# A two-layer graph network: Strassen's second level in o and two more groups, three banks for seven products, and another order of the last group

## The chip, the cores and the metric

The kernel runs on one core of a Trainium2 chip. The core's engines take their instructions in order, each from a queue of its own: TensorE multiplies matrices, VectorE, ScalarE and GpSimd work on elements, SyncE issues the transfers. TensorE writes its results into the accumulators (PSUM), 8 banks of 512 float32 columns in 128 partitions. VectorE and ScalarE read them there. The metric is the device time of one execution in microseconds (us), the median over several runs. All data are float32.

## The reference

x has 64 batches of 256 tokens and 512 features; adj is a 256x256 matrix with zeros and values up to 1. Both layers add their result to x:

```
h = relu(layernorm(x));  x = x + (adj @ h) @ W0 + b0
h = relu(layernorm(x));  q, k, v = h @ Wq + bq, h @ Wk + bk, h @ Wv + bv      (8 heads of 64)
s = q k^T / 8 + (1 - adj) * -1e9;  x = x + softmax(s) v @ Wo + bo
```

The softmax runs over the 256 keys of each head and batch.

## The kernel before

**Groups.** Two batches make a group (GB = 2, NG = 32 groups). Layer 0 runs over all groups and leaves the residual and the transposed hidden state in DRAM; then layer 1 runs over them. In layer 1 the second half of one group is interleaved with the first half of the next. In the loop from line 970 on, iteration g does: attend(g, 0), load_residual(g), load_hidden(g+2), score(g, 1), q and k of group g+1, attend(g, 1), score(g+1, 0), v of g+1, then post(g), which is the product with Wo (o). attend takes four of the eight heads (qd = 0 or 1): the sums over keys (pden), attention times v (pav), and later divide. The last iteration has no next group: it runs post(30) between attend(31, 0) and attend(31, 1), and post(31) at the end.

**Strassen's product.** For a group, w (layer 0), q, k, v and o are each a 512x512 weight times 512 tokens. They are computed by seven products of half size (project, line 447), by Winograd's form: sums of weight quarters (s1 to s4, weight_sums) against differences of the activations' halves (t1 to t4, class Halves, made by GpSimd). Each half product is four matmuls of 128x128 against 128x256 (product, line 439) into one bank. Some products add onto others in a bank: a bank "grows" while VectorE or ScalarE reads its states in between. read() takes a partial sum, finish() completes one quarter of the result.

**The second level.** From group FIRST2 = 4 on, q, k and v use project2 (line 561). Three of the seven half products (a12, s4, a22: those whose result is used in one quarter only) are there computed by Strassen again: seven matmuls of 128x128 against 128x128 in place of eight (product2, line 534). Three or four of the seven write parts of one shared bank, from which VectorE spreads them over the quarters (finish2, line 547). Their weight sums are made once (block_sums, in SBUF that layer 0 has left, `spare`), their activation differences once a group (class Blocks, block_hidden).

**The order of work.** Every step emits its instructions in program order. `after(delay, fn)` puts a function into a list that is due some ticks later, and `tick()`, called after each step of a projection, runs what is due. So a tick decides where, say, a subtraction by GpSimd stands in GpSimd's queue. Banks are taken and given back in first-in, first-out order (bank, give, from line 246 on). The instructions that other parts hang on: top is subtracted from the scores (L846, GpSimd), exp (L851, ScalarE), the key sums `as` (key_sum, L858, GpSimd), which attend's pden needs; reciprocal and product by VectorE in divide (L885, L901); the t sums (L437, GpSimd); bo added to the residual (L978, GpSimd).

**Lines of the page.** L444 is a half product's matmul, L545 a quarter's; L609 is every add of a bank into SBUF by VectorE; L765 and L786 are ScalarE's reads for q, k and for v; L530 to L532 are the differences of the second level. Lines 909 to 915 hold the order of sums and of divide in the last groups:

```
            elif g == NG - 2:
                after(9, HO[g].sums, nc.gpsimd, ("t2", "t3", "t4"))
            else:
                HO[g].sums(nc.vector, ("t2",))
                after(1, HO[g].sums, nc.vector, ("t3", "t4"))

        after(1 if g < NG - 1 or qd else 8, divide)
```

After post(NG-1)'s fourth step the kernel checks its softmax sums for a bound (bad, worst, pf, from line 1004 on) and sets a flag that would start a slower path.

Of the kernel before, what the change touches and what calls it, by code (L numbers as in the profile page):

```python
# [13 lines left out]
P = 128  # L14
# [184 lines left out]
def kernel(  # L199
# [247 lines left out]
    def project(s, halves, by_token, name, read, finish, in_place=False):  # L447

        def new(n):
            return bank([P, 2, N], f"{name}{n}")

        def p1():
            o["a"] = new("a")
            product(o["a"], s, "a11", halves, "b11", by_token, stop=False)
            o["u1"] = read(o["a"], 1)

        def p2():
            pb = new("b")  # L460
            product(pb, s, "a12", halves, "b21", by_token)
            finish(pb, o["u1"], 0, 0)
            give(pb)

        def p3():
            product(o["c"], s, "s4", halves, "b22", by_token, start=False)
            finish(o["c"], o["u2"], 0, 1)
            give(o["c"])

        def p4():  # L470
            pd = new("d")
            product(pd, s, "a22", halves, "t4", by_token)
            finish(pd, o.get("u3"), 1, 0)
            give(pd)

        def p5():
            o["c"] = new("c")
            product(o["c"], s, "s1", halves, "t1", by_token, stop=False)
            o["c22"] = read(o["c"], 0)

        def p6():
            product(o["a"], s, "s2", halves, "t2", by_token, start=False, stop=False)
            o["u2"] = read(o["a"], 2)

        def p7():
            product(o["a"], s, "s3", halves, "t3", by_token, start=False)
            o["u3"] = read(o["a"], 3)
            finish(o["a"], o["c22"], 1, 1)
            give(o["a"])

        o = {}
        for step in (p1, p5, p2, p6, p4, p7, p3) if in_place else (p1, p2, p6, p5, p7, p4, p3):
            step()
            yield

# [5 lines left out]
    FIRST2 = 4  # L501
    W2, spare = {}, []

    def block_sums(n):

        todo = []
        for a in ONCE:
            w = W[n][a]
            def part(i, j):
                return w[:, j, i * P:(i + 1) * P]  # L510
            s1, s2, s3, s4 = (spare.pop(0) for _ in range(4))
            W2[n, a] = dict(a11=part(0, 0), a12=part(0, 1), a22=part(1, 1), s1=s1, s2=s2, s3=s3, s4=s4)
            for o, p, q, op in ((s1, part(1, 0), part(1, 1), ALU.add), (s2, s1, part(0, 0), ALU.subtract),
                                (s3, part(0, 0), part(1, 0), ALU.subtract), (s4, part(0, 1), s2, ALU.subtract)):
                todo.append((nc.gpsimd.tensor_tensor, o, p, q, op))
        return todo
# [17 lines left out]
    def product2(own, shared, s, x, by_token, fresh):  # L534

        q = own.rearrange("p m (n k) -> p (m n) k", k=P)
        c11, c12, c21, c22 = (q[:, i, :] for i in ((0, 2, 1, 3) if by_token else (0, 1, 2, 3)))
        for o, a, b, start in ((shared[:, 0, :], "a11", "b11", True), (shared[:, 1, :], "s2", "t2", False),
                               (shared[:, 2, :], "s3", "t3", False),
                               (c22 if fresh else shared[:, 3, :], "s1", "t1", fresh),  # L540
                               (c11, "a12", "b21", False), (c12, "s4", "b22", False), (c21, "a22", "t4", False)):
            lhs, rhs = s[a], x.operand(b)
            if by_token:
                lhs, rhs = rhs, lhs
            nc.tensor.matmul(o, lhs, rhs, start=start, stop=True, skip_group_check=True)  # L545

    def finish2(o, own, shared, u, by_token, fresh):

        def quarters(t):
            return t.rearrange("p m (n k) -> p (m n) k", k=P)  # L550

        def spread(i, n):
            return shared[:, i:i + 1, :].to_broadcast([P, n, P])
        q = quarters(o)
        lower = q[:, 1::2, :] if by_token else q[:, 2:4, :]
        right = q[:, 2:4, :] if by_token else q[:, 1::2, :]
        return [(o, own, u), (q, spread(0, 4), q), (q[:, 1:4, :], spread(1, 3), q[:, 1:4, :]),
                (lower, spread(2, 2), lower),
                (right[:, 0, :], quarters(own)[:, 3, :], right[:, 0, :]) if fresh else (right, spread(3, 2), right)]

    def project2(n, halves, blocks, by_token, name, read, target):

        s = W[n]

        def new(i):
            return bank([P, 2, N], f"{name}{i}")

        def once(own, a, i, k, u, fresh):
            shared = bank([P, 4, P], f"{name}r")
            product2(own, shared, W2[n, a], blocks[ONCE[a]], by_token, fresh)  # L570
            return own, shared, finish2(target(i, k), own, shared, u, by_token, fresh)

        def finish_all(*products):
            for ops in zip(*(ops for _, _, ops in products)):
                for op in ops:
                    add(*op)
            for own, shared, _ in products:
                give(own)
                give(shared)

        pa = new("a")
        product(pa, s, "a11", halves, "b11", by_token, stop=False)
        u1 = read(pa, 1)
        yield
        pc = new("c")
        product(pc, s, "s1", halves, "t1", by_token, stop=False)
        c22 = read(pc, 0)
        yield
        product(pa, s, "s2", halves, "t2", by_token, start=False, stop=False)
        u2 = read(pa, 2)  # L590
        yield
        c12 = once(pc, "s4", 0, 1, u2, False)
        yield
        c11 = once(new("b"), "a12", 0, 0, u1, True)
        finish_all(c12, c11)
        yield
        product(pa, s, "s3", halves, "t3", by_token, start=False)
        u3 = read(pa, 3)
        add(target(1, 1), pa, c22)
        give(pa)  # L600
        yield
        finish_all(once(new("d"), "a22", 1, 0, u3, True))
        yield

    def partial(name, n):
        return tmp.tile([P, 2, N], F32, tag="u", name=f"u{n}_{name}")
# [4 lines left out]

    RESIDUAL = {0: (1, 1), 1: (0, 0), 2: (0, 1), 3: (1, 0)}
# [30 lines left out]
    def layer0(g):  # L643
# [17 lines left out]
        for d in range(DC):  # L661
# [5 lines left out]
            if d >= 2:  # L667
                halves.sums(nc.gpsimd, ("t1", "t2"), d - 2)
# [9 lines left out]

        def read(ps, n):
            o = quarter(xt, *RESIDUAL[n])  # L680
            add(o, ps, o)
# [20 lines left out]
        def finish(ps, u, i, k):  # L702
            o = quarter(xt, i, k)
            add(o, ps, o)
# [15 lines left out]
        yield from project(W["0"], halves, True, f"w_{g}", read, finish)  # L720
# [14 lines left out]
    def hidden_sums(g, *steps):  # L735

        HH[g] = Halves(f"h_{g}", [H1T[g][:, k] for k in range(GB)], 0 if g else 1)
        for step, n in zip(steps, ("t1", "t2", "t3", "t4")):
            after(step, HH[g].sums, nc.gpsimd, (n,))

    H2 = {}
# [305 lines left out]
```

## Time and profile before

| | us |
|---|---|
| median of 3 runs | 2688.69 (2688.48 to 2688.98) |
| the profiled execution | 2688.09 |
| its span, first to last instruction | 2686.3 |
| TensorE busy (matmuls) | 2659.3 |
| VectorE busy | 1958.6 |
| GpSimd busy | 1960.1 |
| ScalarE busy | 868.9 |

Layer 1 begins about 613 us after the span's start (its first q is interleaved with the end of layer 0), and its groups follow at 63.5 us each from group 4 on. A line of the page names the engine, the operation, what it writes and reads, the shape, the count and the duration. The chain of work is followed backwards from the last instruction: it tells what set the end. A float32 matmul shows as two records of its weight load and two of its product, so x8 on L444 is one half product and x2 on L545 one quarter matmul. Since matmuls are pipelined, the distance of starts is what one costs; the recorded length has the drain in it.

### The profile page before, as it was taken

To read this page: it belongs to the slowest core of one execution; us is meant where nothing else is said; L and a number is where in the kernel's file an instruction comes from. 1 tells how busy PE (TensorE), PEld (TensorE's weight loads), DVE (VectorE), ACT (ScalarE), POOL (GpSimd) and SP (SyncE) were. 2 spreads that over 40 slices of the span, in tenths; PEclk is the share of its full clock that TensorE was granted. 3 is DMA by queue.
4 is the path that set the end of the run, shared out by engine and by line. 5 is a ranking of instruction groups with operands and counts; after the bars stand their busy time and mean duration, and the time that the engine had idled before them with its cause. 6 is when DMAs were issued, how large, how long until landed. Compare 5 with 4: busy or idle time off the path is not lost.

```text
span 2686.3 us, 47911 instructions
## 1 busy us (share of the span) xinstructions
PE 2659.3 (99%) x18684; PEld 2267.5 (84%) x18684; DVE 1958.6 (73%) x3789; ACT 868.9 (32%) x1537; POOL 1960.1 (73%) x1630
## 2 busy tenths in 40 slices
PE   8999999999999999999999999999999999999998
PEld 7888888888788888888888888888888888888886
DVE  7878787875455777777777777777777777777776
ACT  3444344443222233332222233222222333332222
POOL 6777777674777777777777777777777777777775
PEclk9999999999999999999999999999999999999999
DMA  7776666663112221111111111111122211111110
GB/s 188 187 198 162 163 170 166 164 157 97 31 54 61 55 52 48 48 48 48 48 48 48 48 48 48 48 48 48 56 63 63 56 48 48 48 48 48 48 48 33
DMA packets 281047, 210.80 MB, mean 78 GB/s; under 512 B 145904, under 2 KB 212976, under 8 KB 280816
## 3 DMA queue, kind: packets, MB, share of 16 engines
q1 hardware_dynamic: 280352, 207.15, 29.7%
q8 instruction: 150, 2.46, 0.4%
q10 hardware_dynamic: 464, 0.52, 0.1%
q14 instruction: 81, 0.66, 0.1%
HBM read 106.96 MB, written 100.66 MB: 77 GB/s over the span
## 4 chain that ended last, share of the span: by engine, by line
PE 97%; DVE 1%; POOL 1%; DMA 0%; issue 0%; SPq 0%; ACTq 0%; POOLq 0%; DVEq 0%
PE sc L835 8%; PE py L655 8%; PE pav L874 8%; PE pden L867 2%; POOL a L846 1%; DVE v L609 0%; DVE k L609 0%; PE v_29a L444 0%; PE q_29a L444 0%; PE v_28a L444 0%; PE v_27a L444 0%; PE v_25a L444 0%; PE q_25a L444 0%; PE v_24a L444 0%; PE q_23a L444 0%; PE q_21a L444 0%
## 5 line engine op out<-in xcount | busy, mean ns | idle before, releaser
L846 POOL TENSOR_TENSOR a<-a,top 128x1024 f32<-128x1024 f32 x254 | 593.2, 2369 | 512.3 <-DVE a L840 512.3
L840 DVE SCALAR_TENSOR_TENSOR a<-sc,maskT 128x512 f32<-128x512 f32 x512 | 312.0, 682 | 58.1 <-PE sc L835 57.4
L858 POOL TENSOR_TENSOR as<-a 128x512 f32<-128x512 f32 x256 | 319.2, 1281 | 0.7 <-DVE r L691 0.7
L851 ACT ACTIVATE a<-a 128x1024 f32<-128x1024 f32 x256 | 264.1, 1054 | 22.4 <-POOL a L846 22.4
L885 DVE RECIPROCAL den<-den 128x128 f32<-128x128 f32 x256 | 223.7, 919 | 38.0 <-ACT den L881 37.9
L835 PE MATMUL sc<-q,k 64*128 64x256 f32 x2048 | 239.2, 383 | 0.6 <-DVE a L840 0.6
L835 PEld LDWEIGHTS sc<-q,k 64*128 64x128 f32 x2048 | 194.3, 187 | 46.1 <-issue 26.3
L874 PE MATMUL pav<-a,v 128*32 128x256 f32 x4096 | 232.7, 379 | 0.0
L655 PE MATMUL py<-adjT,h 128*128 128x256 f32 x1024 | 228.2, 381 | 0.9 <-DVE adjT L325 0.9
L655 PEld LDWEIGHTS py<-adjT,h 128*128 128x128 f32 x1024 | 195.7, 191 | 28.5 <-ACT h L630 1.2
L874 PEld LDWEIGHTS pav<-a,v 128*32 128x32 f32 x4096 | 133.1, 110 | 87.9
L685 ACT ACTIVATE h<-x,nb,rs 128x512 f32<-128x512 f32 x128 | 97.1, 806 | 318.3 <-POOL nb L54 318.1
L881 ACT ACTIVATE den<-pden 128x512 f32<-128x512 f32 x64 | 38.2, 597 | 493.8 <-PE pden L867 493.1
L53 POOL TENSOR_TENSOR rs<-rs,mhalf 128x2 f32<-128x2 f32 (+1 forms) x97 | 78.8, 812 | 123.7 <-DVE nb L52 123.7
L978 POOL TENSOR_TENSOR x<-x,bo_r 128x512 f32<-128x512 f32 x128 | 159.4, 1277 | 12.2 <-DVE x L609 12.2
L634 POOL TENSOR_TENSOR x<-x,b_r 128x512 f32<-128x512 f32 x128 | 159.1, 1276 | 1.0 <-ACT h L630 0.9
L437 POOL TENSOR_TENSOR t_y<-yT,t_y 128x256 f32<-128x256 f32 (+1 forms) x96 | 87.3, 909 | 41.2 <-ACT yT L665 38.6
L706 DVE BATCH_NORM_STATS2 st<-x 128x6 f32<-128x256 f32 x256 | 96.4, 418 | 4.4
L630 ACT ACTIVATE h<-x,nb,rs 128x512 f32<-128x512 f32 x128 | 93.9, 805 | 10.8 <-POOL nb L54 10.8
L42 DVE BATCH_NORM_STATS2 st<-x 128x6 f32<-128x512 f32 x128 | 85.6, 669 | 7.5 <-DMA x<-in_x_dram 7.5
L437 POOL TENSOR_TENSOR t_y<-yT 128x256 f32<-128x256 f32 (+1 forms) x96 | 88.0, 916 | 2.3 <-ACT yT L665 0.9
L691 DVE STREAM_TRANSPOSE r<-h 128x512 f32<-128x512 f32 x128 | 82.7, 683 | 2.1 <-ACT h L685 1.4
(5610 smaller groups left out, 6381.4 us busy)
## 6 DMA issues: line engine op xcount, KB each, us to landing
x<-in_x_dram SPq DMA_DIRECT2D x256, 128.0 KB, 3.5
residual<-x SPq DMA_DIRECT2D x256, 128.0 KB, 2.3
hidden<-r SPq DMA_DIRECT2D x128, 256.0 KB, 4.6
h1T<-hidden SPq DMA_DIRECT2D x64, 512.0 KB, 9.4
x<-residual SPq DMA_DIRECT2D x32, 1024.0 KB, 6.7
out_dram<-x SPq DMA_DIRECT2D x62, 512.0 KB, 3.2
w_sb<-in_L_gnn_weight_dram SPq DMA_DIRECT2D x1, 1024.0 KB, 6.5
wq_sb<-in_L_gnn_Wq_dram SPq DMA_DIRECT2D x1, 1024.0 KB, 7.7
```

The lines of the kernel that those rows point to most:

```text
L437: eng.tensor_tensor(self.t[n][:, c, :], self.operand(p, c), self.operand(q, c), op=ALU.subtract)
L634: nc.gpsimd.tensor_tensor(xt[:, t, :], xt[:, t, :], b0_r, op=ALU.add)
L655: nc.tensor.matmul(pss[d][:, b * N:(b + 1) * N], h[:, b * NT + k, d * P:(d + 1) * P], adjT[:, k, :], start=(k == 0), stop=(k == NT - 1))
L685: nc.scalar.activation(h1[:, k * NT + t, :], xt[:, k * NT + t, :], AF.Relu, bias=nb[:, t:t + 1], scale=rs[:, t:t + 1])
L835: nc.tensor.matmul(ps[j][:, kt * N:(kt + 1) * N], k[j * HD:(j + 1) * HD, c, kt * P:(kt + 1) * P], q[j * HD:(j + 1) * HD, c, :], start=True ...
L840: nc.vector.scalar_tensor_tensor(a[:, j * NT:(j + 1) * NT, :].rearrange("p k n -> p (k n)"), ps[j], SCALE, maskT_f, op0=ALU.mult, op1=ALU.add)
L846: nc.gpsimd.tensor_tensor(a, a, top_b, op=ALU.subtract)
L851: nc.scalar.activation(a, a, AF.Exp)
L858: nc.gpsimd.tensor_tensor(AS[c, b], a4[:, :, 0, :], a4[:, :, 1, :], op=ALU.add)
L874: nc.tensor.matmul(po[f][h * 32:(h + 1) * 32, b * N:(b + 1) * N], v[:, k, h * HD + f * 32:h * HD + f * 32 + 32], A[h // 2, b][:, (h % 2) * ...
L885: nc.vector.reciprocal(rden[:, c * P:(c + 1) * P], den[:, c * P:(c + 1) * P])
L978: after(9 + t, lambda t, xt: nc.gpsimd.tensor_tensor(xt[:, t, :], xt[:, t, :], L1["o"][1], op=ALU.add), t, X[g])
```

## The change

1. **project** has three banks (pa, pc, pb) and another order: a11, a12, s2, s3, s1, a22, s4. a11, s2, s1 and s4 grow in pa; s3 and a22 in pc; a12 has pb. `put` writes a first value into a quarter of the result (`first`: ScalarE with bias for q and k, a copy for v, an add on VectorE into x for layer 0 and o), `more` adds a bank to it in place.
2. **project2** computes the three inner products in parts: after a11 into pa, s3 into pc and s2 into pa (steps 1 to 3, each read by put) come their a11 products together in step 4 (each into the first 128 columns of a bank of its own), s2 and s3 in step 6, the rest in step 7, and s1 last. The sums grow in those banks, so that VectorE adds each state only to the quarters that want it, and nothing is spread over four.
3. **FIRST2** is 2 instead of 4, and **post** uses project2 from group 2 on (block_outputs, with GpSimd; on VectorE for the last group). Its first value is an add to x on VectorE (add_up).
4. **The inner s3** of a weight is written over the quarter that it is made of. block_sums run at other ticks: q in iteration 0, k and v in iteration 1, o in iteration 2.
5. **t sums** are made in the order t3, t1, t2, t4 (hidden_sums) and t3, t2, t4 (divide); in layer 0, t1 by halves as soon as yT is there.
6. **The last groups**: divide always comes one tick after attend; post(30) is cut at its fifth step by attend(31, 1); sums of o_30 at 5 ticks for 9; OT of the last group lies in the pool of x; only one subtraction of top is left to VectorE, in score(31, 1); that score's key sums and the adds of bo come earlier. exp of a score's fourth part comes two ticks later, except there.
7. **Output**: a batch is sent when its two quarters are complete; in the last group each quarter is sent by itself, and three of the four at the very end.

The core of the diff:

```diff
+        pa = bank([P, 2, N], f"{name}a")
+        product(pa, s, "a11", halves, "b11", by_token, stop=False)
+        put(pa, 0, 0)
+        yield
+        pb = bank([P, 2, N], f"{name}b")
+        product(pb, s, "a12", halves, "b21", by_token)
+        more(pb, 0, 0)
+        give(pb)
+        complete(0, 0)
+        yield
+        product(pa, s, "s2", halves, "t2", by_token, start=False, stop=False)
+        put(pa, 1, 0)
+        yield
+        pc = bank([P, 2, N], f"{name}c")
+        product(pc, s, "s3", halves, "t3", by_token, stop=False)
+        put(pc, 1, 1)
+        yield
+        product(pa, s, "s1", halves, "t1", by_token, start=False, stop=False)
+        more(pa, 1, 1)
+        complete(1, 1)
+        yield
+        product(pc, s, "a22", halves, "t4", by_token, start=False)
+        more(pc, 1, 0)
...
+        product(pa, s, "s4", halves, "b22", by_token, start=False)
+        put(pa, 0, 1)
...
-    FIRST2 = 4
+    FIRST2 = 2
...
+    def project2(n, halves, blocks, by_token, name, place, first, done=None, add_up=False):
...
+        for a, i, k, own in (("a12", 0, 0, None), ("a22", 1, 0, pc), ("s4", 0, 1, pa)):
+            inner.append(Inner(a, i, k, own, bank([P, 2, P], f"{name}{i}{k}")))
+            inner[-1].u1()
+        p2, p4, p3 = inner
+        for p in inner:
+            if p is not p3 or add_up:
+                p.add(p.sum, 0, 0)
+            else:
+                p3.begin(p3.sum, 0, 0)
+        p2.own = pb = bank([P, 2, N], f"{name}b")
+        p2.only((0, 0), (0, 1), (1, 0), fresh=True)
+        for m, n in ((0, N), (1, P)) if add_up else ((slice(0, 3), P),):
...
+            add(o[:, m, 0:n], u[:, m, 0:n], o[:, m, 0:n])
+        give(pb)
+        yield
+        product(pa, s, "s1", halves, "t1", by_token, start=False, stop=False)
+        more(pa, 1, 1)
+        complete(1, 1)
+        yield
+        for p in inner:
+            p.u2()
+            p.s3t3()
+            if p is not p3 or add_up:
+                p.add(p.sum, 1, 0)
+                p.add(p.r, 1, None)
...
+        yield
+        p4.only((0, 0), (0, 1), (1, 0))
+        p3.only((0, 1), (0, 0), (1, 0))
+        more(pc, 1, 0)
+        give(pc)
+        if add_up:
+            more(pa, 0, 1)
...
+        give(pa)
+        for p, c in zip(inner, ((0, 0), (1, 0), (0, 1))):
+            p.u3()
+            p.add(p.sum, None, 1)
+            give(p.shared)
+            complete(*c)
+        yield
...
-        for step, n in zip(steps, ("t1", "t2", "t3", "t4")):
+        for step, n in zip(steps, ("t3", "t1", "t2", "t4")):
...
-                if g == NG - 1 and c + b == 2:
+                if (g, qd) == (NG - 1, 1) and c + b == 2:
...
-                after(3 + 2 * c + b, exponent, a)
+                after((3, 4, 5, 8 if sum_delay > 3 else 6)[2 * c + b], exponent, a)
...
+            eng = nc.gpsimd if g < NG - 1 else nc.vector
+            wait = 5 if g == NG - 2 else 0
+            sums = lambda: HO[g].sums(eng, ("t3", "t2", "t4"))
+            if qd == 0:
+                HO[g].sums(eng, ("t1",))
             else:
-                HO[g].sums(nc.vector, ("t2",))
-                after(1, HO[g].sums, nc.vector, ("t3", "t4"))
-
-        after(1 if g < NG - 1 or qd else 8, divide)
+                if wait:
+                    after(wait, sums)
+                else:
+                    sums()
+                if g >= FIRST2:
+                    block_outputs(g, eng, wait + 2)
+
+        after(1, divide)
...
-    hidden_sums(1, 1, 2, 8, 9)
+    hidden_sums(1, 1, 2, 6, 7)
...
-        score(g, 1, 5)
+        score(g, 1, 5 if g < NG - 1 else 3)
...
-            after(9 + t, lambda t, xt: nc.gpsimd.tensor_tensor(xt[:, t, :], xt[:, t, :], L1["o"][1], op=ALU.add), t, X[g])
+            after((9 if g < NG - 1 else 4) + t, lambda t, xt: nc.gpsimd.tensor_tensor(xt[:, t, :], xt[:, t, :], L1["o"][1], op=ALU.add), t, X[g])
...
-        if g < 3:
-            for i, work in enumerate(block_sums("qkv"[g])):
-                after(4 + i // 2, *work)
+        for n, at in (("q", 7),) if g == 0 else (("k", 1), ("v", 5)) if g == 1 else (("o", 2),) if g == 2 else ():
+            for i, work in enumerate(block_sums(n)):
+                after(at + i // 3, *work)
...
-            run(post(g - 1))
+            last = post(g - 1)
+            run(last, 5)
         attend(g, 1)
...
     tick()
+    run(last)
     last = post(NG - 1)
     run(last, 4)
```

In class Inner, u1, u2 and u3 are the matmuls a11, s2 and s1 into the growing sum, s3t3 the one beside it in the same bank, only the other three; add and begin bring a part of a bank into the quarters of the result, on VectorE and by `first`.

## The prediction

> **What bounds the kernel.** I read the page first: shares, clock, chain.
>
> ```profile
> span 2686.3 us, 47911 instructions
> PE 2659.3 (99%) x18684; PEld 2267.5 (84%) x18684; DVE 1958.6 (73%) x3789; ACT 868.9 (32%) x1537; POOL 1960.1 (73%) x1630
> PEclk9999999999999999999999999999999999999999
> ...
> PE 97%; DVE 1%; POOL 1%; DMA 0%; issue 0%; SPq 0%; ACTq 0%; POOLq 0%; DVEq 0%
> ```
>
> TensorE is busy for all but 27 us, at full clock, and carries 97% of the chain. So the time is the sum of the matmuls plus a few stalls: removing matmuls pays at once, provided that no new wait opens. Next the timeline of TensorE in one steady group (k of group 20), where both kinds of product stand side by side; columns are start, length with the pipeline's drain, instruction.
>
> ```profile
> 1902.04 1.89 PE L444 MATMUL k_20a<-h1T,wk_sb 128*128 128x256 f32 x8
> 1903.77 1.89 PE L444 MATMUL k_20c<-t_h,wk_s 128*128 128x256 f32 x8
> 1905.49 1.89 PE L444 MATMUL k_20a<-t_h,wk_s 128*128 128x256 f32 x8
> 1907.22 0.38 PE L545 MATMUL k_20r<-h1T,wk_s 128*128 128x128 f32 x2
> ...
> 1908.78 0.39 PE L545 MATMUL k_20r<-h1T,wk_sb 128*128 128x128 f32 x2
> ...
> 1910.34 1.89 PE L444 MATMUL k_20a<-t_h,wk_sb 128*128 128x256 f32 x8
> ```
>
> Starts matter here. A plain product takes (1907.22-1902.04)/3 = 1.727 us; a product in seven quarter matmuls (1910.34-1907.22)/2 = 1.560, or 0.223 a matmul. The difference is 0.167 us. No idle time stands between them.
>
> Third, who made TensorE wait, and the stretches around the waits (window, TensorE busy, PEld, DVE, ACT, POOL, clock).
>
> ```profile
> PE pf L1009 <- DVE worst L1007: 3.8, 1, 3.8
> PE o_30a L444 <- POOL t_o L437: 2.8, 1, 2.8
> PE q_1a L444 <- POOL t_h L437: 2.4, 1, 2.4
> ```
>
> ```profile
> 1066.00:2590.00 1524.00, 1524.00 (x12051) 1296.49 (x12050) 1143.95 (x2018) 461.99 (x864) 1142.40 (x818) 1.00 0.19 51
> 2620.00:2650.00 30.00, 27.17 (x222) 22.29 (x218) 25.17 (x40) 11.58 (x16) 23.01 (x13) 1.00 0.00 1
> 2650.00:2686.30 36.30, 25.81 (x164) 19.00 (x162) 20.48 (x30) 2.13 (x6) 11.45 (x9) 0.88 0.17 60
> ```
>
> For 1524 us there is no idle TensorE at all; the waits are in the move between the layers and in the last 66 us.
>
> **What the Trainium skill says.** "PSUM — Partial Sum Buffer", PSUM bank collisions, tells to guard a bank, not an address: a matmul into a bank must wait for every earlier read of that bank. I take each wait so. "TensorE: Matmul & The Clock Gate", LDWEIGHTS, makes the load proportional to its columns; the trace agrees: each record's 128x128 load lasts 190 to 192 ns under either matmul width, so a 128-column matmul is nearly load-bound and cannot fall far below 0.223. The same page, The HAM clock gate, says that an idle window of about 3.4 us halves the clock. Here the 3.8 us wait on L1009 was followed by 0.50, the 2.4 us wait on q_1a by 0.64 to 0.71 (its next two products took 2.79 and 2.84 us where 1.89 is usual), the 2.8 us wait on o_30a by no drop.
>
> **The change, part by part.**
>
> Quarter products. FIRST2 falls from 4 to 2: groups 2 and 3 turn 2 x 3 projections x 3 products = 18. o of groups 2 to 31 turns 30 x 3 = 90. Together 108 x 0.167 = -18.0 us.
>
> Their readers. VectorE's L840 gives 0.61 us for 512 columns back to back (4.88 for eight); an add of 384 columns lasts 0.551 where 512 last 0.684, so 128 columns are 0.133. That is 1.04 ns a column and some 0.076 us an add, so 0.47, 0.34 and 0.21 for 384, 256, 128. For q, k or v, before: s4 with 512+512+384+256+256 columns, a12 and a22 with 512+512+384+256+128 each, one add of 512; 16 adds, 6016 columns, 7.5 us. After: 15 adds (2 and 1 of 128, one of 384, 512, 2x(128+256), 128, 512, 128+256, 3x256), 3712 columns, 5.0 us. For o: 8 adds of 512 (4.9 us) become 20 adds of 5760 columns (7.5). A group saves 3 x 2.5 - 2.6 = 4.9 us of VectorE, which is busy 47 us in 63. ScalarE reads 2048 columns a projection as before. All that hides; what matters is whether each read is over in time.
>
> Margins. Let 0 be a projection's start: pa 0, pc 1.73, pa 3.45, the three first sums and pb 5.18, pa 6.52, sums 8.25, last part 9.58 to 11.6. A read starts some 0.19 after the product's last issue. A load also waits (PEld o_30a stood still as long as o_30a), so a bank must be free 0.2 before its matmul. The tightest is pa at 6.52, read by ScalarE from 5.37: two activations, 0.84, end at 6.21, wanted by 6.31. In q the exp between them moved this read to 5.55-6.39 in the trace while q's first product is 0.1 longer: 6.39 against 6.41. I take +0.5 us over all groups, 0 to 4. In o VectorE reads it at 5.37-5.98. The second sums are read by 9.25 to 11.0, their matmuls are at 10.92, 11.15, 11.37. pa's read at 8.44-9.05 precedes 10.25. All hold. Behind each stand the next reads of the same engine, and with them the banks; each is over well before the following projection takes the bank.
>
> Layer 0 has seven adds for eight. pa's adds end at 6.15 and 9.5; its matmuls come at 6.91 and 10.37. t3, now wanted at step 4, is ready. Worth 0.
>
> GpSimd. o's block sums add, by L530-L532 of h, 1.26+0.72+0.74 and 0.74+0.46+0.46 = 4.4 us a group. After v starts (0): top is subtracted until 8.3, t3, t2, t4 until 12.1, block sums until 16.6, four key sums until 21.5. The next pden is at 23.3, so 1.8 us remain. Then t_h and its blocks until 31.0, where the next subtraction could begin at 30.4; exp has the slack. Cost 0; without that cover each microsecond costs 30. The rows show the room: GpSimd's idle time (in brackets) before the subtractions of group 20.
>
> ```profile
> 1920.85 9.33 POOL L846 TENSOR_TENSOR a<-a,top 128x1024 f32<-128x1024 f32 x4 [11.15 <-DVE a L840]
> 1952.77 6.99 POOL L846 TENSOR_TENSOR a<-a,top 128x1024 f32<-128x1024 f32 x3 [4.35 <-DVE a L840]
> ```
>
> The block sums lie in the tile that holds den and rden. If a wait counts the whole tile, they wait for ScalarE's note, done near 8, and den (wanted at 12.5 of o) for o's last matmul, at 11.6: 0. SyncE's queue: both out transfers of a group now leave at o's end, 3.5 us later for one; behind them load_residual and load_hidden of later groups, landing in 6.7 and 9.4 us and read at least 15 us later: 0.
>
> Weight sums: k's and v's now both lie in group 1's stretch (24 x 0.46 = 11 us); the last key sum ends near 24.2 against 23.9 wanted: +0.3.
>
> Between the layers. Second-layer t2 of group 1 moves ahead of the subtractions: q_1a's 2.4 us and its slow clock, (2.79+2.84-3.78) = 1.85, go. But group 0's list is read in the new order t3, t1, t2, t4, so t2 gets the late tick 16: GpSimd does t_y until 617.5, then t2 until 618.8, while q_0's third product is due at 616.93: +1.9, and a possible slow clock, half of 1.85. A key sum of v_0 is some 0.3 late. Sum -2.4-1.85+1.9+0.9+0.3 = -1.1.
>
> The last groups. Zero is v_31's start (2620.18). All four subtractions are on GpSimd, until 8.3; key sums 0 and 1 until 10.8; then, at tick 6, t3, t2, t4 of o_30 until 14.6, and only then key sums 2 and 3, 15.8 and 17.1. pden(31,0) wants them at 11.8 and 12.4: stall 4.6. Queued behind it on TensorE are pav, the scores and o_30. Scores run 20.9-24.6; VectorE ends them at 26.9, then, since divide now comes at once and not eight ticks later, two reciprocals, two products, t1 (3.6 us) precede o_30's first add, which ends at 31.1. o_30's third product, due at 28.1, waits 3.1. pden(31,1) waits for its last key sum (38.2) and ends at 38.5, where before it ended at 2657.1, that is 36.9. After it, o_30's last matmuls wait 2.3 behind four reciprocals and three sums on VectorE, o_31 twice some 1 us (a late add; the flag). VectorE ends at 62.9, before 61.4: +1.5. Three quarters of out are then sent at once, not one: +1. A slow clock after the 4.6: +2. Together +4.5; bounds 0 (the stalls absorb each other) and +9 (a slow clock after each).
>
> Sum, on the profiled execution's 2688.1: -18.0 +0.5 +0.3 -1.1 +4.5 = 2674.3. The runs' median lies 0.6 above it, so 2675.
>
> **Rivals.**
> 1. The tail gains. Before, from v_31 on it holds 11.7+8.1+12.1+4.5+12.1 = 48.5 us of matmuls in 60.7, 12 us lost; if my stall at pden(31,0) is not there, its 4.6 and the slow clock go: 2668. For it: work of both o's is now spread. Against: GpSimd's row of subtractions and sums is longer than v_31.
> 2. A reader is late in every projection: slower. In o twenty short adds on VectorE stand between matmuls that wait for them; if the adds' completion, not their length, sets the pace, TensorE waits at the second or third sums. The net gain is 13.8 us, so 0.46 us in each of 30 o's cancels it and more makes the kernel slower; 1 us, with 0.2 in each of the 90 other projections, is +48: near 2720. For it: 20 adds instead of 8, margins of 0.1 to 0.5. Against: VectorE loses load, and waits for TensorE 0.4 to 1 us before most adds of o.
> 3. GpSimd is late at pden: if 16.6 is 19 in truth, key sums end at 24 and each group waits; 1 us in each makes 2705. Against: the 15.5 us of idle GpSimd shown above.
> 4. ScalarE's read of pa is 0.1 us late in each q, k and v: 90 x 0.1 = +9, 2684. For it: the margin of 0.02 to 0.1. Against: the first half of the bank is read 0.4 earlier, if that counts.
>
> **How the numbers follow.** Forecast 0.60, own range 2670 to 2682. Rival 1: 0.16; rival 2: 0.12; rival 3: 0.04; rival 4: 0.08, 0.05 of it within 0.2%. A run can tell 0.2% (5.4 us) from no change. Faster: 0.59+0.16+0.03 = 0.78; same 0.01+0.05 = 0.06; slower 0.12+0.04 = 0.16. Leaving out rivals 2 and 3 and rival 4's upper end gives 2666 to 2686.
>
> **What would show it.** Quarter matmuls in o at 0.223 and o taking 11.6 us: step one. No row of idle before matmuls between 1066 and 2550, group period 63.0 for 63.5: the margins. A wait of q_0a on t_h near 1.9, none of q_1a. A wait of pden(31,0) on the key sums near 4, and o_30's on an add near 3. Wrong if a wait repeats in every group.

## The result and the profile after

| | before | after |
|---|---|---|
| median, us | 2688.84 (4 runs, 2688.48 to 2689.47) | 2678.88 (4 runs, 2678.66 to 2680.14) |
| ratio to before | | 0.9964 (95%: 0.9946 to 0.9981) |
| profiled execution | 2688.09 | 2678.95 |
| its span | 2686.3 | 2677.2 |
| v_31's start to the span's end | 66.1 | 73.4 |

The kernel became 10.0 us faster, 0.36% by the ratio. The prediction was 2675 with a range of 2666 to 2686. In the profiled span the gain is 9.1 us where the prediction's sum gave 13.8.

Shares and clock on the page of the kernel after:

```profile
span 2677.2 us, 50551 instructions
PE 2644.4 (99%) x19332; PEld 2278.2 (85%) x19332; DVE 1850.7 (69%) x4096; ACT 901.7 (34%) x1747; POOL 2100.7 (78%) x1829
PEclk9999999999999999999999999999999999999999
```

There are 648 more matmul records, but TensorE is busy for 15 us less. VectorE lost 108 us, GpSimd gained 141. TensorE is still the bound: outside of its busy time lie 33 us, before 27. So it now stands still for longer than it did.

The timeline of TensorE in k of group 20 (start, length, instruction):

```profile
1890.73 1.89 PE L444 MATMUL k_20a<-h1T,wk_sb 128*128 128x256 f32 x8
1892.46 1.89 PE L444 MATMUL k_20c<-t_h,wk_sb 128*128 128x256 f32 x8
...
1895.91 0.39 PE L554 MATMUL k<-h1T,wk_sb 128*128 128x128 f32 x2
1896.13 0.39 PE L554 MATMUL k<-t_h,wk_sb 128*128 128x128 f32 x2
...
1902.42 0.85 PE L912 MATMUL pden<-as,ones 128*32 128x256 f32 x12
```

A plain product takes 1.73 us, a quarter matmul 0.22, k from its first matmul to pden 11.69, all as before. o of group 19 also takes 11.70 (1922.23 to 1933.92), where seven whole products make 12.1 (7 x 1.727). The whole group, q_20 to q_21, lasts 63.00 us (1879.03 to 1942.03); before it lasted 63.48 (1890.34 to 1953.82).

The stretches of the steady state and of the last groups in one table (window, length, then the busy times of TensorE, PEld, DVE, ACT and POOL, the clock, the share of the DMA engines, GB/s):

```profile
1066.00:2570.00 1504.00, 1504.00 (x12433) 1296.30 (x12433) 1041.21 (x2221) 484.41 (x1027) 1238.58 (x955) 1.00 0.19 50
2603.79:2630.00 26.21, 22.15 (x189) 16.76 (x187) 15.09 (x31) 7.74 (x15) 20.73 (x15) 0.93 0.01 1
2630.00:2656.12 26.12, 20.16 (x156) 15.21 (x155) 20.48 (x37) 6.03 (x10) 18.73 (x14) 0.90 0.00 1
2656.12:2677.20 21.08, 13.05 (x77) 11.58 (x76) 12.40 (x33) 0.00 (x0) 0.00 (x0) 0.90 0.29 103
```

As before, the steady state, here 1504 us, passes without idle TensorE. The loss lies behind it: from v_31 on TensorE stands still for 18 of 73 us, 7 of them behind its last matmul, and the clock is below full in all three stretches. Who made it wait:

```profile
PE pden L912 <- POOL as L903: 4.4, 3, 3.5
PE o_30a L444 <- DVE x L655: 3.4, 1, 3.4
PE w_0a L444 <- POOL t_y L437: 2.6, 1, 2.6
PE o L554 <- DVE x L655: 2.0, 1, 2.0
PE q_0a L444 <- POOL t_h L437: 1.8, 1, 1.8
PE pf L1064 <- DVE worst L1062: 1.3, 1, 1.3
```

The wait of q_1a is gone, and no line repeats in every group. The third line (w_0a) was in no part of the prediction. Compared by the starts of named products in the two traces, the 9.1 us come about like this:

| stretch | forecast | measured | from |
|---|---|---|---|
| head, to w_1 | 0 | +3.2 | w_1 begins at 42.81, before 39.58 |
| between the layers, to k_1 | -1.1 | -1.8 | q_0 +2.0, pden(0,0) +0.5, q_1 -4.3 |
| group 4's scores | 0 | -1.4 | k_4 to v_4: 19.80, before 21.22 |
| quarter products to v_31 | -17.0 | -16.4 | 6 projections and 28 o at 0.48 each |
| readers, weight sums | +0.8 | 0 | no wait of TensorE there |
| v_31 to the end, o_30 and o_31 included | +3.5 | +7.3 | 73.4, before 66.1 |
| sum | -13.8 | -9.1 | |

The forecast's -18.0 is shared out here: -17.0 up to v_31, and -1.0 for o_30 and o_31 against its +4.5 for the last groups.

### The profile page after: what moved, and what is told of

Same layout as the page of the kernel before. It is cut to its first block, busy times and chain, and to the rows that moved or that the text cites. A ratio compares the mean times of both kernels' runs of the same rounds, so it can differ in the third digit from the quotient of the medians.

```text
span 2677.2 us, 50551 instructions
## 1 busy us (share of the span) xinstructions
PE 2644.4 (99%) x19332; PEld 2278.2 (85%) x19332; DVE 1850.7 (69%) x4096; ACT 901.7 (34%) x1747; POOL 2100.7 (78%) x1829
## 5 line engine op out<-in xcount | busy, mean ns | idle before, releaser
L896 ACT ACTIVATE a<-a 128x1024 f32<-128x1024 f32 x256 | 270.7, 1058 | 8.2 <-POOL a L891 7.8
L931 DVE RECIPROCAL rest<-rest 128x128 f32<-128x128 f32 x256 | 224.3, 919 | 39.3 <-ACT rest L927 39.3
L726 ACT ACTIVATE h<-x,nb,rs 128x512 f32<-128x512 f32 x128 | 97.1, 806 | 305.9 <-POOL nb L54 305.9
L655 DVE TENSOR_TENSOR k<-k,k 128x128 f32<-128x128 f32 (+1 forms) x300 | 96.1, 352 | 126.2 <-PE k L554 123.9
L927 ACT ACTIVATE rest<-pden 128x512 f32<-128x512 f32 x64 | 38.2, 597 | 419.5 <-PE pden L912 419.5
L655 DVE TENSOR_TENSOR x<-o,x 128x128 f32<-128x128 f32 (+1 forms) x360 | 110.8, 349 | 3.1
L655 DVE TENSOR_TENSOR v<-v,v 128x128 f32<-128x128 f32 (+1 forms) x300 | 95.5, 351 | 15.0 <-PE v L554 11.9
L655 DVE TENSOR_TENSOR q<-q,q 128x128 f32<-128x128 f32 (+1 forms) x300 | 96.1, 352 | 13.9 <-PE q L554 11.8
```

The source lines that it names most:

```text
L655: nc.vector.tensor_tensor(o, ps, u, op=ALU.add)
L726: nc.scalar.activation(h1[:, k * NT + t, :], xt[:, k * NT + t, :], AF.Relu, bias=nb[:, t:t + 1], scale=rs[:, t:t + 1])
L896: nc.scalar.activation(a, a, AF.Exp)
L931: nc.vector.reciprocal(rden[:, c * P:(c + 1) * P], den[:, c * P:(c + 1) * P])
```

## Experiments

Beside these runs the kernel before had medians of 2688.65 to 2689.19 us, so their times can be compared. Where an edit touches one stretch, that stretch is compared within a trace: "head" is w_0's first product to w_1's, "tail" is v_31's start to the span's end. The kernel after has 22.1 and 73.4. These vary between executions of the same instructions. In nine traces whose head is that of the kernel after, it takes 21.8 to 22.2 us four times and 23.1 to 23.6 five times; in the five the clock fell after the wait in w_0. In five traces with the tail of the kernel after it takes 73.1 to 74.9. A difference has to be larger than that to count.

### The head: bias additions ahead of t1

```diff
-    ready(0, (0, 0, 2, 2), (0, 2), (1, 1, 3, 3), (5, 5, 6, 6), batches=2)
+    ready(0, (0, 0, 2, 2), (0, 2), (1, 1, 3, 3), (4, 4, 4, 4), batches=2)
```

> The changed kernel, but the four bias additions of group 0 on GpSimd come at step 4, ahead of the first half of t1, and not at steps 5 and 6 behind it. Theory (GpSimd runs in order; t1's first half waits 4.8 us for yT, and the four additions, 5.9 us, wait behind it): the sums of y then stand one after the other from 19 us on, the 2.6 us wait of w_0's third product goes and w_1 begins 3.1 us earlier, at 39.7 for 42.8; nothing later takes it back: 2675.8. Rival (the late weights, which came at 15.1 us for 13.4, or the slower VectorE sum of the weights set the third product): the wait stays at 1 us or more, 2677 to 2679.

GpSimd's timeline at the start, first of the kernel after:

```profile
18.96 0.73 POOL L437 TENSOR_TENSOR t_y<-yT 128x256 f32<-128x256 f32 x1 [4.81 <-ACT yT L711]
19.64 2.95 POOL L680 TENSOR_TENSOR x<-x,b_r 128x512 f32<-128x512 f32 x2
22.55 0.72 POOL L437 TENSOR_TENSOR t_y<-yT 128x256 f32<-128x256 f32 x1
23.24 2.93 POOL L680 TENSOR_TENSOR x<-x,b_r 128x512 f32<-128x512 f32 x2
26.14 1.40 POOL L437 TENSOR_TENSOR t_y<-yT,t_y 128x256 f32<-128x256 f32 x2
```

and of this kernel:

```profile
14.63 5.41 POOL L680 TENSOR_TENSOR x<-x,b_r 128x512 f32<-128x512 f32 x4
20.00 1.42 POOL L437 TENSOR_TENSOR t_y<-yT 128x256 f32<-128x256 f32 x2
21.37 1.41 POOL L437 TENSOR_TENSOR t_y<-yT,t_y 128x256 f32<-128x256 f32 x2
```

In the kernel after, GpSimd waits 4.81 us (in brackets) for yT, with four additions behind the waiting sum that could have run; t2 (the last row) is ready at 27.5 and not at 22.8. Measured: 2675.34 us, ratio to before 0.9948 (0.9931 to 0.9964); head 19.3, the wait gone. In this execution the weights happened to be early too: VectorE's first sum of them began at 13.1 us, in the kernel after at 15.1. So this trace alone doesn't exclude the rival, late weights. Two traces of further experiments do: with the additions in the late place and that sum at 13.0, TensorE still waits 2.3 us (the run with o_30 and o_31 in whole products); with the additions moved and that sum at 15.4, nothing waits and the head takes 19.0 (the last run with quarter products). The cause of the 3 us is shown.

### Between the layers: t3 late in place of t2

```diff
-            hidden_sums(0, 1, 2, 16, 16)
+            hidden_sums(0, 16, 1, 2, 16)
```

> The changed kernel, but of group 0's hidden sums t1 and t2 come early and t3 takes the late place, in the list of steps between the layers. Theory: GpSimd's late sum then ends at 622.0, where q_0's fourth product wants it at 621.9 to 621.7, so 1.8 us of wait become 0.2 to 0.4: -1.6, 2677.3. Rival (GpSimd's row there is the bound, whichever sum comes first): the wait moves to q_0's fourth product whole, 2678.5 to 2679.

Measured: 2678.39 us (ratio 0.9958, 0.9944 to 0.9972). q_0 takes 12.40 us for 14.11, so 1.7 less, as expected, and no wait of 0.3 us or more is left in it. The median fell by only 0.5, and the profiled execution not at all: its head was 1.0 us and its tail 0.8 us longer than in the kernel after, within what these stretches vary. The 1.7 us are shown by the stretch alone.

### All o in whole products

```diff
-        if g < FIRST2:
+        if True:
             yield from project(W["o"], halves, True, f"o_{g}", place, add_to, done)
...
-                if g >= FIRST2:
-                    block_outputs(g, eng, wait + 2)
```

> The changed kernel, but every o in seven whole products again, and the block sums of o left out; q, k and v of groups 2 and 3 stay in quarter products. Theory (a quarter matmul is 0.223 us, nothing waits for the short adds of o): each o of groups 2 to 29 takes 3 x 0.167 = 0.50 us more, so v_31 begins 28 x 0.49 = 13.7 us later than the 2603.8 of the changed kernel, at 2617.5; the stretch from there to the end changes by +1.0 for o_30 and o_31, less what the missing 4.4 us of block sums give back: 2690 to 2694 in all. Rival 2 (the 20 short adds cost TensorE time): the loss is smaller than 13.7, since the adds go too, or there is none.

The block sums of o's weights still write over one quarter of three weight blocks here, so o multiplies partly by other weights; instructions and shapes are as described. Measured: 2686.79 us, ratio 0.9994 (0.9985 to 1.0003). v_31 begins at 2616.49, and q_0 began 0.8 us earlier than in the kernel after: 28 o cost 13.5 us, 0.48 each, as the quarter products promise. The 20 short adds of an o cost TensorE nothing in the steady state; rival 2 is wrong there. The tail, however, is 67.4 us for 73.4, so the run ended 3 us below the 2690 that were expected at least. In the last groups the quarter products *cost*.

### Only o_30 and o_31 in whole products

```diff
-        if g < FIRST2:
+        if g < FIRST2 or g >= NG - 2:
             yield from project(W["o"], halves, True, f"o_{g}", place, add_to, done)
...
-                if g >= FIRST2:
+                if FIRST2 <= g < NG - 2:
                     block_outputs(g, eng, wait + 2)
...
+                if g == NG - 3:
+                    for a in ONCE:
+                        s3, a11 = W2["o", a]["s3"], W2["o", a]["a11"]
+                        after(13, nc.gpsimd.tensor_tensor, s3, a11, s3, ALU.subtract)
```

> The changed kernel, but o_30 and o_31 in seven whole products; GpSimd restores the three weight quarters that the block sums had overwritten, in its idle time during k of group 31 (3 x 0.46 us). Theory (from the run with every o plain, whose stretch from v_31's start to the end was 6.0 us shorter than the changed kernel's: o_31 began 4.3 us and the end came 6.0 us earlier against v_31): v_31 begins at 2603.8 as in the changed kernel, o_31 4 us earlier, the end 6 us earlier, 2672.5 to 2673.5. The step of the prediction that put o_30 and o_31 into the sum as -1.0 is then wrong in sign. Rival (those 6 us came from something else that every o plain brings, such as GpSimd's freed time in the groups before): the end gains less than 2 us, 2677 or more.

Measured: 2673.05 us, ratio 0.9943 (0.9928 to 0.9958), tail 67.5. o_30's start to o_31's takes 22.2 us for 26.1, o_31's to the end 19.2 for 21.1. The sign of the step "o_30 and o_31: -1.0" was wrong: they cost 5.9. The waits of TensorE say by what:

```profile
PE pden L912 <- POOL as L903: 4.0, 2, 3.5
PE o_30a L444 <- DVE x L655: 3.4, 1, 3.4
```

The two long ones are still there. The 2.0 us wait of the growing-sum matmul ("o L554 <- DVE x") is gone, with the slow clock that followed it and the third wait of pden. And after TensorE's last matmul 5.2 us pass, not 6.8.

### o_30's sums behind the key sums

```diff
-            wait = 5 if g == NG - 2 else 0
+            wait = 7 if g == NG - 2 else 0
...
-                    block_outputs(g, eng, wait + 2)
+                    block_outputs(g, eng, wait + (0 if wait else 2))
```

> The changed kernel, but in the last groups t3, t2, t4 of o_30 come on GpSimd behind the last two key sums of v_31's stretch, and its block sums right after them; the last block sums, of t4, come one step later, behind the subtractions. Theory: the wait of pden(31,0), 3.5 + 0.6 us, and the slow clock after it, 1.4 us, go; o_30 begins 5.3 us earlier, at 22.2 us after v_31's start (26.2 in the changed kernel, less the 1.4); the subtractions start 1 to 2 us late and give back up to 2 us at pden(31,1) or at o_30's sums of t4. In all -2 to -5: 2674 to 2677. Rival (VectorE is the bound of the last groups): o_30's third product waits longer by what pden gains, and the end does not move, 2678 to 2680.

Measured: 2676.6 us, ratio 0.9952 (0.9935 to 0.9968). The tail is 68.9, so 4.5 less; o_30 begins 21.5 us after v_31 and not 26.2. pden's waits fall from 4.4 to 1.3 in sum, and nothing later takes it back. The row of sums on GpSimd ahead of the key sums was the cause of the stall, as the prediction had it.

### The division of (31,0) at once

```diff
-        after(1, divide)
+        if (g, qd) == (NG - 1, 0):
+            divide()
+        else:
+            after(1, divide)
```

> The changed kernel, but the division of (31,0) is given to VectorE at once, ahead of the reading of the next scores, and not one step later, behind it. Theory (o_30's third product waits because two reciprocals, two products and t1, 4.0 us, stand on VectorE between the scores and o_30's first add): this work falls into VectorE's idle 3.0 us before the scores, whose reading is 0.9 to 1.6 us late; the 3.4 us wait of o_30's third product falls to 0.7 to 1.5, and the slow clock after it, 1.5 us, goes: -2.5 to -4, 2675 to 2676.5, from o_30's fourth step on. Rival (the key sums of (31,1) set the pace there): what o_30 gains, pden(31,1) waits more for GpSimd, by 2 us or more, and the end does not move.

Measured: 2680.88 us, ratio 0.997 (0.9958 to 0.9982); tail 74.5, inside the 73.1 to 74.9 that it has without the edit. So nothing was gained; a loss isn't shown. The waits:

```profile
PE pden L912 <- POOL as L903: 8.8, 4, 3.5
...
PE o_30a L444 <- DVE x L655: 0.4, 1, 0.4
```

o_30's wait did fall from 3.4 to 0.4, and TensorE reaches pden(31,1) 3.2 us earlier after v_31's start (36.8 for 40.0). But GpSimd's last key sum ends no earlier, at 41.7 for 41.4, and pden now waits 1.8, 1.8 and 1.7 us for the sums; pav after it runs at a low clock (5.9 us for 3.8). The expectation failed; the rival, GpSimd's chain to pden(31,1), is right. Easing one engine moved the wait to the other.

### All of it together, with whole and with quarter products at the end

On top of the edits above (o plain in the last two groups only), the sums of o_31 come one tick later, t1 of o_31 two to three ticks later, and the flag's product (pf) one step later.

```diff
-                if wait:
-                    after(wait, sums)
+                if wait or g == NG - 1:
+                    after(wait or 1, sums)
...
+    run(last, 1)
     pf = bank([1, 1], "pf")
```

> All together, on the changed kernel: group 0's bias additions at step 4; t3 of group 0's hidden sums late in place of t2; o_30 and o_31 in whole products; o_30's sums behind the key sums; the division of (31,0) at once, its t1 two steps later; the sums of o_31 behind o_30's next adds; the flag's product one step later. Theory: the single gains are head 2.8, t3 1.7, plain 6.0, keys 4.6, division 2.5; the last three overlap in part, since each takes one wait of the last groups: 9 to 12 us for the last groups, so 2678.9 - 4.5 - 10 = 2664, 2662 to 2668. Rival (VectorE's total in the last groups sets the end): the last groups gain 6 us, no more than plain products alone: 2668 or more.

> The same as the run with all mends together, but o_30 and o_31 in quarter products as in the changed kernel; o_30's block sums, all three groups of them, stand behind its sums (the last, of t4, one step later). Theory: the mends give the last groups 6 to 9 us, and the 20 adds for 8 of the two o's cost VectorE 2.6 us each where VectorE sets the pace: 2 to 4 us slower than the version with whole products: 2665 to 2671. Rival (order alone was at fault in the last groups, not the short adds): as fast as the version with whole products or 1 us faster.

Measured: with whole products in o_30 and o_31 **2663.17 us** (2662.74 to 2663.31), ratio to before 0.9906 (0.9891 to 0.9921); with quarter products 2668.45, ratio 0.9927 (0.9914 to 0.9941). The first is the fastest version of this study, 15.7 us below the kernel after. Its tail by the same three stretches:

```profile
2598.96:2620.47 21.51, 20.51 (x188) 16.47 (x186) 17.02 (x33) 8.47 (x17) 17.25 (x12) 1.00 0.00 2
2620.47:2642.49 22.02, 18.17 (x139) 14.30 (x138) 16.26 (x22) 5.53 (x8) 18.11 (x11) 1.00 0.00 1
2642.49:2660.50 18.01, 12.56 (x59) 10.45 (x57) 7.07 (x13) 0.00 (x0) 0.00 (x0) 0.91 0.33 119
```

That is 61.5 us for 73.4, with the clock full until o_31. The version with quarter products has 68.0: a difference of 6.4 in the tail and 5.3 in the medians, where 2 to 4 were expected. The waits of the two, whole products first:

```profile
PE pden L912 <- POOL as L903: 3.2, 3, 1.8
PE o_30a L444 <- DVE x L655: 1.6, 2, 1.2
```

```profile
PE pden L912 <- POOL as L903: 4.9, 4, 1.8
PE o_31a L444 <- DVE x L655: 2.2, 1, 2.2
PE o_30a L444 <- DVE x L655: 2.0, 2, 1.6
```

So order alone was not at fault. Nor does VectorE's total set the end: the last groups gained 11.9 us, and that rival had allowed 6. VectorE is busy for 40 of the 61.5 us with whole products and for 49 of the 68.0 with quarter products. It isn't full in either, but TensorE waits for single adds on it, behind reciprocals, products and t sums. The quarter products put 2.6 us of adds on it for each o, as the prediction counted, and 2.5 us of o_31's block sums. GpSimd carries 4.2 us more (35.4 and 39.6), o_30's block sums, and feeds pden later. Which of these loads costs how much of the 6.4 us, no run separates.

### Is there room on GpSimd?

The second kernel has range(2).

```diff
         O2[g] = block_sums_of(x, t, HO[g], t4, eng, step)
+        if g < NG - 2:
+            for _ in range(1):
+                after(step + 1, HO[g].sums, eng, ("t4",))
```

> The changed kernel with one more 512-column subtraction on GpSimd in each of groups 2 to 29: t4 of o computed a second time, with the same numbers, behind the block sums, ahead of the four key sums. Theory (GpSimd's row was free because 1.8 us lay between the last key sum, 1932.13, and the pden that wants it, 1933.92): 1.24 us more fit in; no wait of pden opens, the time stays at 2679, 1 either way. Rival 3 of the prediction (GpSimd at 78% is the bound, the margin is not there): 0.5 us or more a group, 14 us or more, 2693.

> The same with two more such subtractions a group, 2.46 us. Theory: 2.46 less the 1.8 of margin is 0.66 us of wait of pden on the key sums in each of 28 groups: +18 us, 2697, and perhaps half a microsecond more a group for four key sums that come one by one. If the margin is wider than it looks, since what follows is late too and the next group starts from there, the loss is under 5 us.

Measured: 2713.94 us (ratio 1.0093, 1.0076 to 1.011) and 2767.24 (ratio 1.0292, 1.0275 to 1.0309). Both expectations failed, and not by way of pden:

```profile
PE o L554 <- POOL t_o L437: 24.6, 28, 0.9
...
PE pden L915 <- POOL as L906: 3.9, 2, 3.4
```

The addition was badly placed: it writes t4 again, and o's fourth step reads t4 already 5.4 us after o's start. TensorE waits 0.88 us for it in each of 28 groups (24.6 in sum). So the margin of 1.8 us ahead of pden was not tested and stays argued only. What the runs do show is the price of a wait that repeats. In the first, 0.88 us of wait cost 32 us in 28 groups (the two traces at v_31, less their difference at q_2), 1.1 each. In the second, 2.2 us of wait cost 3.1 each: the clock fell after it in 10 of the 28 groups, and a group with the fall lasts 67.2 us, one without 65.5.

### Does a reader's lateness count at once?

```diff
         product(pa, s, "s2", halves, "t2", by_token, start=False, stop=False)
         put(pa, 1, 0)
+        if not add_up:
+            put(pa, 1, 0)
         yield
```

> The changed kernel, but in q, k and v of groups 2 to 31 ScalarE's second reading of the bank pa (two activations, 0.84 us, in q and k, one copy, 0.59 us, in v) is done twice, with the same result. Theory of the margins (the next matmul into pa waits until the bank's last reading is over; q_21's reading ended at 1948.35, the matmul came at 1948.65): the second reading ends 0.5 us after the matmul's time in q and k, 0.1 to 0.2 in v: 0.55 + 0.55 + 0.15 = 1.2 us a group, 30 groups: +36 us, 2700 to 2725 with what ScalarE passes on. If only the half of the bank that is written next counts, the waits stay under 0.3 us, +20 us or less; if there is slack that the start times do not show, 0.

Measured: 2722.36 us, ratio 1.0124 (1.0107 to 1.014). Between the starts, q is 0.6 us longer, k 0.6, v 0.2: 1.4 a group against 1.2 expected, 43.5 us in all. Had only the half of the bank that is written next counted, it would have been 20 or less. In q of group 20:

```profile
1911.24 1.57 ACT L818 ACTIVATE q<-q_20a,bq_c 128x256 f32<-128x256 f32 x4
...
1912.86 1.59 PEld L444 LDWEIGHTS q_20a<-t_h,wq_s 128*128 128x128 f32 x8 [0.51 <-ACT q L818]
```

The reading ends at 1912.81 and the next weight load into this bank's product begins 0.05 later. That agrees with the Trainium skill, "PSUM — Partial Sum Buffer", PSUM bank collisions raise a hardware error (guard by bank, not by address), and with the way the prediction read its margins: a reader that is late by its margin plus x costs about x, in every projection.

### What made group 4 faster

This one edits the kernel before.

```diff
-        early = 2 if g >= FIRST2 and (g, qd) != (NG - 1, 1) else 4
+        early = 2 if g >= 2 and (g, qd) != (NG - 1, 1) else 4
```

> The kernel before, but with two of the four reciprocals of a softmax sum kept back for the next step from group 2 on, not from group 4 on: the condition that FIRST2 also decides. Theory (v_4 began 1.42 us later against k_4 in the kernel before than in the changed one, since four reciprocals of group 3, 3.4 us, stood on VectorE ahead of the scores' reading): the wait of the scores of group 4 on VectorE goes, v_4 begins 1.4 us earlier, the rest is as before: 2687.4. Rival (the quarter products of group 4 or noise made those 1.42 us): no change.

Measured: 2688.35 us, ratio 0.9998 (0.9989 to 1.0007): in the medians not to be seen. In the trace it is. VectorE and the scores in group 4 of the kernel before:

```profile
900.43 3.38 DVE L885 RECIPROCAL den<-den 128x128 f32<-128x128 f32 x4
...
904.41 1.72 PE L835 MATMUL sc<-q,k 64*128 64x256 f32 x8 [0.57 <-DVE a L840]
```

and in this kernel:

```profile
901.00 1.75 DVE L885 RECIPROCAL den<-den 128x128 f32<-128x128 f32 x2
901.54 3.32 PEld L835 LDWEIGHTS sc<-q,k 64*128 64x128 f32 x32 [0.41 <-issue]
901.54 3.73 PE L835 MATMUL sc<-q,k 64*128 64x256 f32 x32
```

With two reciprocals in place of four the scores run without a break, v_4 begins 19.80 us after k_4 as in the kernel after, and o_3 begins 1.4 us earlier against q_4. So 1.4 us of the change's gain come from a condition on FIRST2 that has nothing to do with products.

## Why the prediction was right or wrong

**The sum: inside the range, with misses of both signs.** The head (+3.2) and the last groups (3.8 more than forecast) cost 7.0 us that weren't foreseen, and the quarter products gave 0.6 less. Group 4 (1.4), the readers (0.8) and the move between the layers (0.7) gave 2.9 more than forecast. The direction rests on the quarter products, which were priced rightly. That the sum missed by only 4.7 us is in part luck.

**Quarter products: right.** 0.167 us a product was forecast. Measured are 0.48 us a projection or o, 0.161 a product, and the group lasts 63.0 us as forecast. Whole products in o alone cost 13.5 us in 28 groups.

**Margins: right, with one left open.** No wait repeats. ScalarE's reading of pa cost 0 and not 0.5: it ended 0.3 us ahead of the matmul. Delaying it showed that the margin was read rightly and was small. VectorE lost 3.9 us a group (47.6 to 43.7), forecast 4.9; GpSimd gained 4.4, as forecast. The margin at pden was not tested.

**The weight loads: read wrongly.** The prediction takes a load as proportional to its columns. In the trace of the kernel before it is not: loads of pav with 32 columns (L874) last 110 ns on average, those of py with 128 columns (L655) 191. And the loads of neighbouring quarter matmuls start 0.11 us apart and overlap, so the length of one says little about how fast such matmuls can follow one another. No term of the sum rests on this.

**Between the layers: right.** q_1 gave 4.3 us (4.25 forecast; seen in the trace, no run takes this edit alone), q_0's wait came with 1.8 (1.9) and cost 2.0 in all. The slow clock put beside it (0.9) did not come.

**"Layer 0 ... t3, now wanted at step 4, is ready. Worth 0": wrong.** The step looked at t3 and at VectorE's adds, and in the other groups of layer 0 it holds: from w_1 to q_0 both traces take 573.9 us. It did not follow the moved halves of t1 through GpSimd's queue in group 0, where four bias additions fell behind a sum that waits. Cost 3.2 us; moving the additions back brought the head to 19.3 us, for 19.0 in the kernel before.

**FIRST2's other use: not seen.** The condition on early reciprocals gave 1.4 us.

**The last groups: mechanism right, sizes off.** Forecast and measured, in us: stall at pden(31,0) 4.6 and 4.1; o_30's third product 3.1 and 3.4; its last matmuls 2.3 and 2.0; the flag about 1 and 1.3. The mis-sized term is "a slow clock after the 4.6: +2". The clock fell after three waits: to 0.75 over 5.0 us, 0.56 over 3.9, 0.60 over 4.3, which is 4.7 us of lost full-speed time. The second miss is pden(31,1): its last key sum ended 41.4 us after v_31's start, not 38.2, with pav at a slow clock before it and, on GpSimd, one of the bias additions moved ahead (1.3 us). How much each adds was only read from the trace. With o_30 and o_31 counted in, +7.3 was measured for +3.5. And these two o, booked as a gain of 1.0, cost 5.9 in this order and 6.4 in a better one.

**Rivals.** Rival 1 (the tail gains) did not happen, though a tail of 61.5 us was to be had with another order and whole products in o_30 and o_31. Rivals 2 and 3 did not happen. Rival 4's mechanism is real, but its margin was not used up.

## What to carry to other kernels

- A saving of matmuls pays where TensorE is the bound and its readers have margin. At the end of this program, where TensorE waits for single adds and sums, the same exchange of matmuls for adds cost 6 us: try the form with the fewest adds for the last tiles.
- When an operation moves to an earlier place in a queue, ask what stands behind it while it waits for its input, in the first and last groups apart from the steady ones.
- Two engines that feed the same matmuls have to be eased together. In the last groups the early division alone gave nothing, the order of GpSimd's sums 4.5 us and whole products 5.9; all together, with o_31's sums and the flag moved as well, gave 11.9.

## What was not expected of the hardware

The clock gate. The Trainium skill, "TensorE: Matmul & The Clock Gate", What's actually happening, speaks of an idle window of about 3.4 us that runs freely and isn't restarted by the program. Here shorter waits were enough, but not always. In the kernel with two additions on GpSimd the same wait, 2.16 to 2.25 us, stands in 28 groups. In 18 of them the next whole product took its usual 1.89 us; in 10 it took 3.4 to 3.6. Two groups that follow each other, the matmul behind the wait and the next whole product:

```profile
1915.29 0.49 PE L554 MATMUL o<-wo_sb,t_o 128*128 128x128 f32 x2 [2.22 <-POOL t_o L437]
...
1916.51 1.89 PE L444 MATMUL o_18a<-wo_s,t_o 128*128 128x256 f32 x8
...
1980.77 0.49 PE L554 MATMUL o<-wo_sb,t_o 128*128 128x128 f32 x2 [2.23 <-POOL t_o L437]
...
1982.05 3.51 PE L444 MATMUL o_19a<-wo_s,t_o 128*128 128x256 f32 x8
```

The mean clock was 1.00 behind the first wait and 0.63 over 4.6 us behind the second. Even one wait of the same instructions goes either way: w_0's, in the kernel after and in the kernel with o_30's sums behind the key sums.

```profile
26.91 2.25 PE L444 MATMUL w_0a<-w_s,t_y 128*128 128x256 f32 x8 [2.61 <-POOL t_y L437]
```

```profile
27.49 3.61 PE L444 MATMUL w_0a<-w_s,t_y 128*128 128x256 f32 x8 [2.63 <-POOL t_y L437]
```

The clock was 1.00 over the next 2.1 us in the first and 0.52 over 3.4 us in the second. A free-running window fits that; no run here settles it. So a wait of about 2 us or more has to be priced with a chance of losing more: in these two kernels and the kernel after some 1.2 to 1.8 us of full speed each time the clock fell, which it did in 10 of 28 cases of the one wait and 5 of 9 of the other.

VectorE beside GpSimd: in the head of the kernel after, VectorE's 512-column sums of the weights took 1.47 and 1.76 us while GpSimd ran its bias additions, and 0.69 while GpSimd was idle. In the kernel before, the one beside the bias additions took 0.93, so the size varies. "GPSIMD Engine Reference", Specifications, says that the two share their SBUF interfaces when VectorE has two SBUF inputs.
